# A two-layer graph attention kernel on one core: norm statistics by VectorE instead of TensorE transposes, first-layer weights by ScalarE, new issue lists

## The chip, the core and the metric

The kernel runs on one core of one Trainium2 chip. Its engines work side by side, each on its own queue: TensorE (PE in the profile, with its weight loads as PEld) multiplies matrices, VectorE (DVE) and ScalarE (ACT) work elementwise, GpSimd (POOL) does some sums, and SyncE (SP) issues nearly all of the DMAs. The metric is the device time of one execution in microseconds; the median of the runs counts.

## The reference

The input is `x` of 64 graphs x 256 nodes x 512 features and `adj` of 64 x 256 x 256, all float32. Two layers are applied, the second of which holds two attentions.

```python
# layer 0, 8 heads of 64
Q, K, V = x @ W_q + b_q, x @ W_k + b_k, x @ W_v + b_v
scores = Q K^T / 8 + a_i + c_j + b_g + log(adj + 1e-9)
x = softmax(scores) @ V + x
# layer 1
def layer_norm(x): return (x - mean) * rsqrt(var + 1e-6) * g + b
def graph_attention(x, bias, W, a_src, a_dst):
    h = x @ W                                   # split into heads
    e = leaky_relu(s_i + t_j, 0.2) + bias        # s = h . a_src, t = h . a_dst
    return softmax(e) @ h
attn = graph_attention(layer_norm(x), adj, W1, ...) + x        # 8 heads
out  = graph_attention(layer_norm(attn), adj, W2, ...) + attn  # 1 head
```

## The kernel before

One graph passes through a chain of 42 named steps, written as a Python generator `graph(b)`, which stops after each step. A list says which graph takes its next step when. In the steady part this list is `period`: an entry `(age, name)` lets the graph that is `age` graphs behind the newest take the step `name`, so five or six graphs are under way at once, each in another stage. `start` and `finish` are lists of their own for the two ends. TensorE executes in exactly the order of these lists. The other engines get an order from the scheduler of the framework, which starts what it takes to be ready; each engine then executes its queue strictly in that order.

The steps of one graph are these.

- `load`, `turn`: x and adj come in by DMA, are transposed by VectorE in blocks of 32 x 32 (L471), and lie with features on the partitions (`xT`, tiles of 128 x 4 x 256).
- `V`, `Q`, `K`: three products with 512 x 512 weights, each by a Strassen-Winograd scheme of seven block products (`winograd`; L306 and L313). `V 7`, `V 4` and the like are the last two products of a scheme. GpSimd makes its left sums (`left_factors`, L282 to L285). ScalarE copies intermediate PSUM banks (L495, L528, L607), VectorE adds (L507, L537, L545, L616).
- `scores`, `mask`, `sums 0`, `product 0`, `gather 0`: score products (L562), Exp by ScalarE out of PSUM (L569), multiplication by adj (L583) and sum over key blocks (L588) on VectorE, column sums by TensorE (L362), weighted values by TensorE (L394), and the division and the addition to the residual on VectorE (L403, L408). The inverse sums go through DRAM to reach all partitions. The residual goes to DRAM (`store`) and comes back (`fetch`).
- `tokens 1`: the reciprocal standard deviation of layer norm for each token. TensorE transposes the residual (L249), ScalarE takes the sum and the squares with accumulator (L264, L266), VectorE scales (L270), GpSimd raises to the power -0.5 (L272). The mean itself and g, b are folded into the weights once at the start (`fold_norm`).
- `V1`, `rows 1`, eight times `weights`, `sums 1`, `product 1`, `gather 1`: the first attention of layer 1. The weights are exp(leaky_relu(s+t)+adj), up to a factor that cancels: ScalarE takes Exp of adj plus 0.2 t (L647), VectorE multiplies by the larger of exp(-0.8 s) and exp(0.8 t) (L650).
- `tokens 2`, `V2`, `rows 2`, `weights 2`, twice `product 2`: the second attention with one head. The residual `X2`, in token order, is a by-product of the transposes in `tokens 2` (L264, with the constant row added by GpSimd at L669); L711 multiplies, L718 divides and adds, and L727 sends the result out.

VectorE and GpSimd also keep extremes of intermediate values (`note`, L345, L379, L380). At the end they are compared with bounds; a value outside leads to a slower plain version of the whole computation, which does not run with these inputs.

[...] In SBUF, tiles with one tag share a fixed number of slots: the layer-0 and layer-1 weights `ET` share four, and the temporary `product` of `fold_norm` uses the same four.

Of the kernel before, what the change touches and what calls it, by code (L numbers as in the profile page):

```python
# [15 lines left out]
H = 8  # L16
# [4 lines left out]
def kernel(  # L21
# [46 lines left out]
    top = const.tile([P, P + 4 * H], F32, name="top")  # L68
    bottom = const.tile([P, 4 * H], F32, name="bottom")
    added = const.tile([P, P], F32, name="added")  # L70
# [4 lines left out]
    for t in (top, bottom, added):  # L75
        nc.gpsimd.memset(t, 0.0)
# [9 lines left out]
    nc.gpsimd.memset(eights, 1.0)  # L86

# [57 lines left out]
    with ExitStack() as main:  # L145
# [13 lines left out]
        def fold_norm(name, w, g, b, sources, targets, heads):  # L159
# [9 lines left out]
            for a in (sources, targets):  # L169
                row = data.tile([P, D], F32, name="vector", tag="X2", bufs=4)  # L170
                nc.sync.dma_start(out=row, in_=a.rearrange("h d -> (h d)").partition_broadcast(P))
                vectors.append(row.rearrange("p (n f) -> p n f", n=2))
            for kk in range(2):
                blocks = w[:, kk, :4, :HD].rearrange("p (k n) f -> p k n f", n=2)
                for i, row in enumerate(vectors):
                    product = work.tile([P, 2, 2, HD], F32, name="product", tag="ET", bufs=4)
# [10 lines left out]
            left = data.tile([P, 2, KC, 32], F32, name="left", tag="X2", bufs=4)  # L187
# [10 lines left out]
            sums = data.tile([P, HD + H], F32, name="sums", tag="sums")[:, : HD + more]  # L198
# [11 lines left out]
            if name == "2":  # L210
                row = const.tile([P, D], F32, name="bw")
                nc.sync.dma_start(out=row, in_=stored[0].partition_broadcast(P))
# [31 lines left out]
        def tokens(xT):  # L244

            for t in range(NT):
                pt = ps("tr")
                for kc in range(KC):
                    nc.tensor.transpose(  # L249
                        pt[:, kc * P : (kc + 1) * P], xT[:, kc, t * P : (t + 1) * P], ident  # L250
                    )
                yield t, pt

        def rstd_of(xT, keep=None):

            total, less, squares = (
                small.tile([P, NT], F32, name=n, tag=n) for n in ("total", "less", "squares")
            )
            for t, pt in tokens(xT):
                to = pt  # L260
                if keep:
                    to, pt = keep(t), pt.rearrange("p (k a r) -> p k a r", k=KC, a=4)
                of = slice(t, t + 1)
                nc.scalar.activation(to, pt, AF.Identity, accum_out=total[:, of])  # L264
                nc.scalar.mul(less[:, of], total[:, of], -1.0 / D)
                nc.scalar.activation(  # L266
                    pt, pt, AF.Square, bias=less[:, of], accum_out=squares[:, of]
                )
            var = small.tile([P, NT], F32, name="var", tag="var")
            nc.vector.tensor_scalar(var, squares, 1.0 / D, 1e-6, ALU.mult, ALU.add)  # L270
            rstd = small.tile([P, NT], F32, name="rstd", tag="rstd")
            nc.gpsimd.tensor_tensor(rstd, var, mhalf.to_broadcast([P, NT]), ALU.pow)  # L272
            return rstd
# [68 lines left out]
        def note(v):  # L342
            n = v.shape[1]
            for kept, op in ((top[:, P:], ALU.max), (bottom, ALU.min)):
                nc.vector.tensor_tensor(kept[:, :n], kept[:, :n], v, op)  # L345

        def note_odd(v, low, high):

            bad = data.tile([P, v.shape[1]], F32, name="bad", tag="X2", bufs=4)
# [6 lines left out]
        def weight_sums(totals):  # L356
# [22 lines left out]
            nc.vector.tensor_tensor(top[:, :P], top[:, :P], pt[:, :P], ALU.max)  # L379
            nc.gpsimd.tensor_tensor(added, added, inverse, ALU.add)  # L380
            return R

        def weigh(pair, V, R, xT, bias):
# [17 lines left out]
            for q in (1, 0):  # L401
# [4 lines left out]
                for m in range(2):  # L406
                    k = 2 * q + m
                    nc.vector.scalar_tensor_tensor(  # L408
                        xT[:, k, :], both[:, m, :], bias[:, k : k + 1], xT[:, k, :],
                        ALU.add, ALU.add,  # L410
                    )
# [664 lines left out]
```

## Time and profile before

| what | value |
|---|---|
| time, median of 3 runs | 3303.91 us (3302.41 to 3306.08) |
| profiled execution: time | 3304.79 us |
| profiled execution: span of the core | 3303.0 us |
| TensorE busy | 3208.0 us, 97% |
| VectorE busy | 2488.2 us, 75% |
| ScalarE busy | 1761.0 us, 53% |
| GpSimd busy | 899.5 us, 27% |
| moved by DMA | 340.91 MB, mean 103 GB/s |
| granted TensorE clock | 0.991 of full speed |

The span reaches from the first to the last instruction of the core; the time of the execution has 1.8 us around it. Busy time of an engine is the time in which at least one of its instructions was running. The ends of matmuls are modelled, so for TensorE the distances from start to start are the safer reading. Groups of instructions are named by line: L394 is line 394 of the kernel before.

### The profile page before, as it was taken

What the parts mean: (1) busy time and instruction counts of PE and PEld (TensorE: products, weight loads), DVE (VectorE), ACT (ScalarE), POOL (GpSimd) and SP (SyncE); (2) the same over time, 40 slices, a digit from 0 to 9 for tenths busy, and PEclk for the clock granted to TensorE, in tenths of its full rate; (3) what the DMA queues carried; (4) which work ended last, traced back from release to release, by engine and by line L of the source; (5) the groups of instructions that cost most, each with busy time, mean ns of one, the idle gap of its engine ahead of it and who ended that gap; (6) DMA issues with size and microseconds to landing.
All of it is one profiled execution on the core that took longest, in us unless ns stands there. A gap on an engine that the chain in (4) does not pass through costs nothing.

```text
span 3303.0 us, 76975 instructions
## 1 busy us (share of the span) xinstructions
PE 3208.0 (97%) x29000; PEld 2686.9 (81%) x29000; DVE 2488.2 (75%) x5267; ACT 1761.0 (53%) x4807; POOL 899.5 (27%) x1244
## 2 busy tenths in 40 slices
PE   6899999999999999999999999999999999999997
PEld 4688888888888888888888888888888888888875
DVE  4667777777777777787777777777777777777775
ACT  2455555555555555555555555555555555555553
POOL 2222222322322322322322322322222222222222
PEclk8999999999999999999999999999999999999998
DMA  4324333333333333343343343343343333333322
GB/s 121 105 80 112 106 97 104 109 103 104 106 107 103 105 108 103 97 115 102 98 116 101 97 112 104 93 116 104 93 118 100 98 113 105 98 107 110 99 91 69
DMA packets 271656, 340.91 MB, mean 103 GB/s; under 512 B 108577, under 2 KB 187569, under 8 KB 271281
## 3 DMA queue, kind: packets, MB, share of 16 engines
q1 hardware_dynamic: 270512, 335.40, 36.1%
q8 instruction: 232, 3.80, 0.5%
q14 instruction: 144, 1.17, 0.1%
q10 hardware_dynamic: 768, 0.54, 0.1%
HBM read 233.48 MB, written 102.31 MB: 102 GB/s over the span
## 4 chain that ended last, share of the span: by engine, by line
PE 80%; ACT 10%; DVE 3%; DMA 3%; issue 2%; SPq 1%; POOL 1%; ACTq 0%; DVEq 0%; POOLq 0%
PE ps_a L306 18%; PE ps_num L394 12%; PE ps_a L313 10%; PE ps_b L306 9%; PE ps_sc L562 7%; PE ps_av L711 6%; ACT ET L647 6%; PE ps_c L306 4%; PE ps_su L362 4%; PE ps_b L313 3%; PE ps_tr L249 3%; ACT m L528 2%; DMA R<-kept 2%; PE ps_c L313 2%; ACT u L528 1%
## 5 line engine op out<-in xcount | busy, mean ns | idle before, releaser
L650 DVE SCALAR_TENSOR_TENSOR ET<-R,f,ET 128x256 f32<-128x256 f32 x1024 | 468.3, 496 | 243.4 <-ACT ET L647 214.7
L647 ACT ACTIVATE ET<-AT,lift 128x256 f32<-128x256 f32 x1024 | 442.6, 505 | 172.0 <-PE ps_num L394 172.0
L394 PE MATMUL ps_num<-ET,V 128*32 128x256 f32 x8192 | 466.6, 380 | 0.0
L394 PEld LDWEIGHTS ps_num<-ET,V 128*32 128x32 f32 x8192 | 264.0, 110 | 155.1 <-issue 1.3
L583 DVE TENSOR_TENSOR ET<-ET,AT 128x1024 f32<-128x1024 f32 x256 | 305.2, 1227 | 112.3 <-ACT ET L569 112.3
L569 ACT ACTIVATE ET<-ps_sc,V 128x512 f32<-128x512 f32 x512 | 303.1, 702 | 101.5 <-PE ps_sc L562 90.2
L380 POOL TENSOR_TENSOR added<-added,inverse 128x128 f32<-128x128 f32 x128 | 60.1, 470 | 891.7 <-DVE inverse L368 891.7
L306 PE MATMUL ps_a<-w,S 128*128 128x264 f32 (+1 forms) x1024 | 278.6, 395 | 9.0 <-ACT m L607 8.7
L306 PE MATMUL ps_b<-w,S 128*128 128x264 f32 (+1 forms) x1024 | 267.0, 383 | 0.1
L711 PE MATMUL ps_av<-V,ET 128*128 128x258 f32 (+1 forms) x1024 | 246.6, 385 | 5.7 <-DVE ET L699 5.7
L306 PEld LDWEIGHTS ps_a<-w,S 128*128 128x128 f32 x1024 | 183.4, 190 | 71.9 <-ACT m L607 24.8
L562 PE MATMUL ps_sc<-QT,KT 64*128 64x256 f32 x2048 | 240.0, 384 | 0.0
L562 PEld LDWEIGHTS ps_sc<-QT,KT 64*128 64x128 f32 x2048 | 193.7, 188 | 41.5 <-issue 20.9
L282 POOL TENSOR_TENSOR S<-yT 128x256 f32<-128x256 f32 x64 | 54.5, 851 | 626.2 <-PE ps_su L362 556.9
L306 PEld LDWEIGHTS ps_b<-w,S 128*128 128x128 f32 x1024 | 193.9, 189 | 31.5 <-issue 0.5
L711 PEld LDWEIGHTS ps_av<-V,ET 128*128 128x128 f32 x1024 | 187.1, 193 | 29.1 <-issue 4.6
L272 POOL TENSOR_TENSOR rstd<-var,mhalf 128x2 f32<-128x2 f32 x128 | 90.6, 708 | 284.7 <-DVE var L270 278.2
L282 POOL TENSOR_TENSOR S<-zT 128x256 f32<-128x256 f32 x63 | 45.8, 727 | 445.5 <-DVE zT L408 419.2
L403 DVE TENSOR_TENSOR ps_num<-ps_num,R 128x512 f32<-128x512 f32 x256 | 165.1, 690 | 1.7 <-DMA R<-kept 1.0
L266 ACT ACTIVATE ps_tr<-ps_tr,less 128x512 f32<-128x512 f32 x256 | 165.8, 648 | 0.1
L306 PE MATMUL ps_a<-wv,xT 128*128 128x257 f32 x512 | 142.2, 400 | 22.0 <-ACT ET L569 11.6
L669 POOL TENSOR_TENSOR X<-X,bw 128x512 f32<-128x512 f32 x128 | 159.6, 1267 | 5.7 <-ACT X L264 5.7
(167 smaller groups left out, 7022.8 us busy)
## 6 DMA issues: line engine op xcount, KB each, us to landing
R<-kept SPq DMA_DIRECT2D x128, 512.0 KB
X<-in_x_dram SPq DMA_DIRECT2D x256, 128.0 KB
kept<-xT SPq DMA_DIRECT2D x64, 512.0 KB
yT<-kept SPq DMA_DIRECT2D x64, 512.0 KB
R<-kept SPq DMA_DIRECT2D x512, 64.0 KB
kept<-yT SPq DMA_DIRECT2D x64, 512.0 KB
out_dram<-X SPq DMA_DIRECT2D x512, 64.0 KB
zT<-kept SPq DMA_DIRECT2D x63, 512.0 KB
```

Source lines behind the costliest of these rows:

```text
L266: nc.scalar.activation(pt, pt, AF.Square, bias=less[:, of], accum_out=squares[:, of])
L306: nc.tensor.matmul(to, A[:, kk, :], B[:, kk, :], start=(first and kk == 0), stop=(kk == 1), skip_group_check=not first,)
L313: nc.tensor.matmul(to[:, m * P : (m + 1) * P], B[:, kk, m * P : (m + 1) * P], A[:, kk, :], start=(first and m == kk == 0), stop=(kk == 1), ...
L394: nc.tensor.matmul(num[32 * a : 32 * a + 32, m * N : (m + 1) * N], V[:, j, a // 2, a % 2 * P + q * DH + 32 * m :][:, :32], pair[a // 2][:, ...
L403: nc.vector.tensor_tensor(both, both, R[:, q, :].unsqueeze(1).to_broadcast([P, 2, N]), ALU.mult)
L562: nc.tensor.matmul(banks[h % 2][:, o : o + N], KT[lo : lo + DH, (q + h) // 2, j * P : (j + 1) * P], QT[lo : lo + DH, (q + h) // 2, :], sta ...
L569: nc.scalar.activation(ET[:, j, i::2, :], banks[i].rearrange("p (h n) -> p h n", n=N), AF.Exp, bias=c[:, j, :],)
L583: nc.vector.tensor_tensor(ET[:, j, :, :], ET[:, j, :, :], AT[:, j, :].unsqueeze(1).to_broadcast([P, 4, N]), ALU.mult,)
L647: nc.scalar.activation(ET[:, j, h, :], AT[:, j, :], AF.Exp, bias=lift[:, j, at : at + 1])
L650: nc.vector.scalar_tensor_tensor(ET[:, j, h, :], R[q][:, h, :], f[:, j, at : at + 1], ET[:, j, h, :], ALU.max, ALU.mult,)
L669: nc.gpsimd.tensor_tensor(X2[t], X2[t], folded["2"].row, ALU.add)
L711: nc.tensor.matmul(av[:, :width], ET[:, j, t * P : (t + 1) * P], V2[:, j, n, :width], start=(j == 0), stop=(j == NT - 1),)
```

## The change

Six things are altered.

1. `rstd_of` no longer transposes on TensorE. VectorE turns the residual in 32 x 32 blocks (one instruction of 1024 elements), takes `bn_stats` of eight blocks, and one narrow product with a constant matrix `same` (48 columns) sums what belongs to one token over the partitions; ten or so narrow VectorE instructions make the variance of it. It is split in two by a generator: the first half is traced at `gather`, the second at `tokens`.
2. The first-layer weights are made as Relu on ScalarE, an addition of adj on VectorE (two heads at a time), and Exp on ScalarE, in place of Exp and L650.
3. `weigh` adds two blocks at a time; the bias is added beforehand by ScalarE on the fetched tile (`fetch_biased`).
4. The extremes are replaced by sums that ScalarE accumulates (`note`), and a further check, `skew`.
5. `X2` is made of the block-turned tile Z, plus the constant row on GpSimd, and goes through DRAM into token order. The output is scaled by ScalarE and added by GpSimd in place of L718.
6. `product` of `fold_norm` uses other slots, half of W_q is loaded by ScalarE's queue, and `start`, `period` and `finish` are new lists; graphs are up to five behind the newest in `period`.

```diff
-        def rstd_of(xT, keep=None):
...
-            for t, pt in tokens(xT):
...
-                nc.scalar.activation(to, pt, AF.Identity, accum_out=total[:, of])
-                nc.scalar.mul(less[:, of], total[:, of], -1.0 / D)
-                nc.scalar.activation(
-                    pt, pt, AF.Square, bias=less[:, of], accum_out=squares[:, of]
-                )
+        def rstd_of(xT):
+            Z = data.tile([P, 2 * KC, P], F32, name="Z", tag="Z")
+            nc.vector.transpose(
+                Z.rearrange("p b (k r) -> p k b r", k=KC), xT.rearrange("p k (b r) -> p k b r", r=32)
+            )
+            parts = small.tile([P, 2 * KC, 2, 3], F32, name="parts", tag="parts")
+            for block in range(2 * KC):
+                nc.vector.bn_stats(parts[:, block].rearrange("p h c -> p (h c)"), Z[:, block, :])
+            mean = parts[:, :, :, 1]
+            nc.vector.tensor_tensor(parts[:, :, :, 0], mean, mean, ALU.mult)
+            yield Z
+            pt = ps("st")[:, : 12 * KC]
+            nc.tensor.matmul(
+                pt, same.rearrange("p c r -> p (c r)"), parts.rearrange("p b h c -> p (b h c)"),
+                start=True, stop=True,
+            )
...
+            nc.vector.tensor_tensor(skew, skew, square, ALU.max)
+            nc.vector.tensor_scalar(var, var, 1e-6, None, ALU.add)
             rstd = small.tile([P, NT], F32, name="rstd", tag="rstd")
             nc.gpsimd.tensor_tensor(rstd, var, mhalf.to_broadcast([P, NT]), ALU.pow)
-            return rstd
+            yield rstd
...
+        def note(v, f=AF.Square):
+            n = next(slots[f])
+            unused = small.tile([P, P], F32, name="unused", tag="unused", bufs=1)[:, : v.shape[1]]
+            nc.scalar.activation(unused, v, f, accum_out=seen[:, n : n + 1])
...
+        def fetch_biased(kept, tag, bias):
+            xT = fetch(kept, tag)
+            for k in range(KC):
+                nc.scalar.activation(
+                    xT[:, k, :], xT[:, k, :], AF.Identity, bias=bias[:, k : k + 1]
+                )
+            return xT
...
-                for m in range(2):
-                    k = 2 * q + m
-                    nc.vector.scalar_tensor_tensor(
-                        xT[:, k, :], both[:, m, :], bias[:, k : k + 1], xT[:, k, :],
-                        ALU.add, ALU.add,
-                    )
+                of = xT[:, 2 * q : 2 * q + 2, :]
+                nc.vector.tensor_tensor(of, both, of, ALU.add)
...
                         nc.scalar.activation(
-                            ET[:, j, h, :], AT[:, j, :], AF.Exp, bias=lift[:, j, at : at + 1]
+                            ET[:, j, h, :], R[q][:, h, :], AF.Relu, bias=f[:, j, at : at + 1]
                         )
-                        nc.vector.scalar_tensor_tensor(
-                            ET[:, j, h, :], R[q][:, h, :], f[:, j, at : at + 1], ET[:, j, h, :],
-                            ALU.max, ALU.mult,
-                        )
+                    if h % 2 == 1:
+                        for j in range(NT):
+                            two = ET[:, j, h - 1 : h + 1, :]
+                            nc.vector.tensor_tensor(
+                                two, two, AT[:, j, :].unsqueeze(1).to_broadcast([P, 2, N]), ALU.add
+                            )
+                            for i in (h - 1, h):
+                                nc.scalar.activation(
+                                    ET[:, j, i, :], ET[:, j, i, :], AF.Exp,
+                                    bias=targets[:, j, 4 * q + i : 4 * q + i + 1],
+                                )
...
+            kept = dram.tile([P, 2 * KC, P], F32, name="kept", tag="keptz")
+            nc.gpsimd.tensor_tensor(
+                Z, Z, folded["2"].row.unsqueeze(1).to_broadcast([P, 2 * KC, P]), ALU.add
+            )
+            nc.sync.dma_start(out=kept, in_=Z)
+            yield
+            rstd = next(stats)
+            X2 = data.tile([P, NT, D], F32, name="X2", tag="X2", bufs=2)
+            for q in range(4):
+                for t in range(NT):
+                    nc.sync.dma_start(
+                        out=X2[32 * q : 32 * q + 32, t, :].rearrange("r (a f) -> r a f", a=4),
+                        in_=kept.rearrange("(a r) (t q) f -> t q r a f", a=4, t=NT)[t, q],
+                    )
...
-                    nc.vector.scalar_tensor_tensor(
-                        o[:, cols], av[:, :HD], rinv[:, t : t + 1], o[:, cols],
-                        ALU.mult, ALU.add,
-                    )
+                    weighted = work.tile([P, HD + H], F32, name="weighted", tag="kept", bufs=4)[:, :HD]
+                    nc.scalar.activation(weighted, av[:, :HD], AF.Copy, scale=rinv[:, t : t + 1])
+                    nc.gpsimd.tensor_tensor(o[:, cols], o[:, cols], weighted, ALU.add)
...
-                    product = work.tile([P, 2, 2, HD], F32, name="product", tag="ET", bufs=4)
+                    product = data.tile([P, 2, 2, HD], F32, name="product", tag="R", bufs=3)
...
         period = [
+            (1, "V4"), (2, "mask"), (5, "V2"), (5, "V2 7"), (2, "sums 0"),
+            (2, "product 0"), (5, "V2 4"), (1, "Q"), (5, "rows 2"), (4, "sums 1"),
+            (3, "weights"), (2, "gather 0"), (3, "weights"), (3, "weights"),
+            (5, "weights 2"), (3, "weights"), (0, "turn"), (1, "Q7"), (4, "product 1"),
+            (1, "Q4"), (1, "K"), (1, "K7"), (5, "product 2"), (1, "K4"), (3, "weights"),
+            (5, "product 2"), (2, "tokens 1"), (0, "V"), (1, "scores"), (3, "weights"),
+            (3, "weights"), (2, "V1"), (4, "gather 1"), (-1, "load"), (2, "V1 7"),
+            (0, "V7"), (4, "tokens 2"), (2, "V1 4"), (1, "scores"), (1, "mask"),
+            (2, "rows 1"), (2, "weights"),
         ]
```

## The prediction

> **What bounds the kernel now.** I read busy shares first, then the table of windows, then the timeline of TensorE (PE), and last what PE waits for between 300 and 3000 us.
>
> ```profile
> PE 3208.0 (97%) x29000; PEld 2686.9 (81%) x29000; DVE 2488.2 (75%) x5267; ACT 1761.0 (53%) x4807; POOL 899.5 (27%) x1244
> PE   6899999999999999999999999999999999999997
> ```
>
> PE is busy for 97%, and only the ends of the slice row dip. The windows (PE, PEld, DVE, ACT, POOL busy) say where the other 95 us lie:
>
> ```profile
> 0.00:25.00 25.00, 12.96 (x51) 9.44 (x52) 9.80 (x18) 3.79 (x9) 4.47 (x24) 1.00 0.53 139
> 25.00:50.00 25.00, 14.57 (x125) 13.34 (x123) 7.95 (x16) 4.71 (x13) 5.02 (x5) 0.90 0.65 177
> ...
> 300.00:1300.00 1000.00, 994.29 (x9052) 837.53 (x9051) 769.08 (x1626) 550.65 (x1504) 275.93 (x384) 1.00 0.37 105
> ```
>
> In the steady part PE idles 5.7 us in 1000. The first 300 us lose 49, everything after 3100 us about 33. "Busy" PE isn't PE at its peak, so I check starts. In TensorE's timeline (start, duration) one transpose step looks so:
>
> ```profile
> 1622.71 3.64 PE L394 MATMUL ps_num<-ET,V 128*32 128x256 f32 x64
> 1626.28 1.09 PE L249 MATMUL ps_tr<-ident,yT 128*128 128x128 f32 x8
> 1627.21 1.06 PE L313 MATMUL ps_a<-xT,wq 128*128 128x128 f32 x8
> ...
> 1639.20 1.06 PE L313 MATMUL ps_b<-S,wk 128*128 128x128 f32 x8
> 1640.09 1.04 PE L249 MATMUL ps_tr<-ident,zT 128*128 128x128 f32 x8
> 1640.97 1.06 PE L313 MATMUL ps_a<-S,wk 128*128 128x128 f32 x8
> ```
>
> Groups follow one another without a hole. Start to start, the transposes take 0.93 and 0.88 us, 1.81 us per graph. The page's busy figures for L249 (70.6 + 65.8 us over the run, 2.13 per graph) count overlapping tails, so I use 1.81. The chain of waits shows the score products (L562) starting at 1301.13 and at 3096.91, 36 graphs later: a period of 49.9 us. Hence PE's issue order, written by hand, is the clock, and what PE waits for in it is small:
>
> ```profile
> PE ps_a L313 <- ACT u L528: 10.9, 54, 0.5
> PE ps_a L306 <- ACT m L607: 3.8, 8, 1.3
> ```
>
> Per graph the other engines have 38.4 (DVE), 27.5 (ACT) and 13.8 us (POOL) of the 49.9.
>
> [...] the new 512-wide adds are about 690 ns, which L403 at that width also shows. [...] the POOL sums on yT have median 852 ns and reach 1238, those on zT sit at 727.
>
> **The change part by part**, per graph, for two layers.
>
> *PE.* It removes 16 transposes: -1.81 us. It adds two products of 48 columns. In the trace each f32 product leaves two records (L562: 16 calls, 32 records), a transpose one, so these are four weight loads and four short matmuls. A 128-wide pair is spaced 111 ns (L313: 0.89 us for 8). [...] 4 x 111 = 0.45 us. Bounds: 0.16 if loads hide completely (48 columns at L306's 217 ns per 257 are 41 ns), 1.0 if both steps leave a hole of 0.3 us. Net -1.36 us, period 48.5; times 64: **-87 us** (-52 to -106).
>
> *DVE.* Removed: L650 468.3, L718 121.1, L408 211, L270 75.7, L345 82, L379 29 us over the run: 987, or 15.4 per graph. Added: 8 pair adds x 0.65 = 5.2 (690 ns less the overlap that L403 has, 645); 4 adds in weigh x 0.65 = 2.6, in place of eight L408; 2 block transposes of 1024 elements: L471 takes 680 ns for 512, thus 1.18 each, 2.4; 16 bn_stats of 128 elements. [...] L379, 128 wide, is 225 ns; a pass that reduces (L181, 1221 ns for 1024) scaled down is 288. I take 250, 4.0 us; from 3.2 up to 8 if it needs two passes. Some 20 narrow instructions at the 155 to 200 ns of L683 and L345 are 3.2; the heads' sources scaled on DVE 0.2. Sum 17.6; DVE goes 38.4 -> 40.6 of 48.5 us, 84% (up to 92%). Cost nothing as long as PE is the clock.
>
> *ACT.* Removed: L647, both activations with accumulator, `less`, their reads, two small Exps: 928 us, 14.5 per graph. Added: 16 Relu and 16 Exp at 0.43 = 13.8; 8 bias additions on the fetched tile 3.5; four notes of 128 columns with accumulator (0.30 + 0.19) 2.0, two small ones 0.8; four scaled copies from PSUM at 0.47 = 1.9. Sum 22.0; 27.5 -> 35.0 us, 72%. Hidden under PE too, but here lies the new wait: before, ACT only fed DVE (Exp, then L650). Now Relu on ACT, the add on DVE, Exp on ACT: an Exp at the head of ACT waits for DVE, and behind it queue the copies of PSUM banks (L528, L607) that PE's next product needs. PE's slack there is one group, 0.87 us, and already 0.2 us short at L528. I allow 0.2 us per graph, +13 us (from 0 to 70).
>
> *POOL.* Less L669 and L380 (3.4 per graph), plus one 1024-wide addition at L177's 2.27 and four 256-wide at 0.73: 13.8 -> 15.6 us, 32%. Hidden[...]. The power of -0.5 stays where it was.
>
> *SP and DMA.* One more store of 512 KB and eight loads of 64 KB: 41 -> 50 issues a graph at some 0.43 us (L727: four in 1.74), +3.9 us. SP waits for a landing before the X2 loads, 5 to 6 us by the chain's R<-kept; behind them stand x, adj and R loads. Bytes grow from 341 to 408 MB, DMA share from 0.37 to about 0.46. X2 is read only after V2, rows 2 and weights 2, many microseconds later, and R is asked for several steps ahead of its use. Cost nothing; without that cover, up to 5 us for a late R.
>
> *Start.* In the timeline ACT stands still at the first scores, because `product` of the weight folding takes ET slots:
>
> ```profile
> 51.49 4.73 ACT L569 ACTIVATE ET<-ps_sc,V 128x512 f32<-128x512 f32 x8 [11.34 <-DVE w L181]
> 52.23 1.36 PEld L306 LDWEIGHTS ps_a<-wv,xT 128*128 128x128 f32 x4 [12.03 <-ACT ET L569]
> 52.23 2.08 PE L306 MATMUL ps_a<-wv,xT 128*128 128x257 f32 x4 [11.63 <-ACT ET L569]
> ```
>
> The change puts `product` in R's slots, idle by then, and folds later. I take **-10 us** (0 to -20); what is late next is the fold's DMA chain.
>
> *End.* The last graph's weights step has no cover: 16 Exps of 0.43 under L650 were 7.5 us, 32 activations are 13.8; an output tile passes ACT and POOL (0.47 + 0.73) instead of DVE (0.48); against it stands a shorter norm. **+7 us** (0 to +15).
>
> *Rest.* The notes at their new place, the odd-value checks and memsets at the edges: a microsecond either way.
>
> Sum against the profiled execution: 3303 - 87 + 13 - 10 + 7 = 3226 us of span, plus its own 1.8 around the span, less 0.9 to the median shown: about **3227 us**.
>
> **Rivals.**
> 1. *PE keeps the beat with small holes* (above): 3195 to 3265.
> 2. *Queue coupling eats half.* DVE at 84% and ACT at 72% answer PE late in all five winograd products of a graph, some 0.2 us each: 1 us per graph, +64 instead of +13: 3278. For it: L528's wait in 54 of 54 graphs. Against it: DVE at 77% cost PE almost nothing, and the new lists place products between Q and Q7.
> 3. *Slower: the Relu, add, Exp round trip becomes the clock.* A graph has four head pairs. If ACT stands d us per pair until DVE, busy with masks of 1.2 us, has added, ACT's period is 35.0 + 4d. It passes PE's 48.5 at d = 3.4 and the old 49.9 at d = 3.7; at d = 4.0 it is 51.0, +70 us: 3374. Against it: one mask or sum ahead costs 1.2 to 2.5, and ACT has other graphs' work.
> 4. *PE does not shrink*: transposes hidden under weight loads. The start-to-start reading speaks against it: with the additions elsewhere about 3305.
>
> **How the numbers follow.** Chances: rival 1 0.62, 2 0.22, 3 0.12, 4 0.04. A difference of 0.2%, 6.6 us, is about what can be told from no change; faster means below 3297, slower above 3311. Rival 1 and nearly all of 2 are faster: 0.83; 4 and the edge of 2 about unchanged: 0.04; slower 0.13. The likeliest is 3227. The range 3185 to 3285 takes rival 1 with the better bounds of start and PE, and most of 2.
>
> **What would show it.** PE still at or above 96%; the score products every 48.5 us; two short groups of two pairs each where L249 stood, near 0.22 us apart; DVE near 40 and ACT near 35 us per graph; the ACT wait at the first scores gone. It is wrong if PE falls under 94% in the steady windows with PE waiting for ACT copies (rivals 2 and 3), if bn_stats is far above 300 ns, or if SP waits for the Z store make R late.

## The result, and the profile after

The changed kernel takes **3262.89 us** (median of 4 runs, 3258.05 to 3264.86) against 3304.99 us (4 runs, 3302.41 to 3306.84) of the kernel before: ratio 0.9871, 95% interval 0.9854 to 0.9888. The forecast was 3227 us, 3185 to 3285. So it is 1.3% faster, inside the range, with 42 us gained of the 77 that the sum had promised. The profiled execution took 3264.86 us, its span is 3263.1 us; what follows is read from it, against the 3303.0 us before.

The page's first two parts, engine totals (busy us, share, instructions) and the slice row of TensorE:

```profile
PE 3172.2 (97%) x28232; PEld 2604.9 (80%) x28232; DVE 2700.9 (83%) x6093; ACT 2192.0 (67%) x5959; POOL 1077.0 (33%) x1315
PE   7999999999999999999999999999999999999985
```

TensorE is still at 97%, and the row dips only at its ends. VectorE has 213 us more, ScalarE 431, GpSimd 178, and hardly any of it shows in the middle. The table of windows of the changed kernel (columns as before):

```profile
25.00:50.00 25.00, 22.07 (x156) 19.28 (x158) 14.12 (x24) 9.00 (x22) 3.81 (x4) 1.00 0.59 157
300.00:1300.00 1000.00, 995.08 (x8994) 822.39 (x8994) 844.77 (x1914) 698.09 (x1910) 331.42 (x404) 1.00 0.41 128
```

TensorE idles 4.9 us in the steady 1000 (5.7 before). In the first 300 us it idles 30.8 us (48.4 before); after 3100 us it idles 49 us (31 before). **The ends cancel**: about 18 us won at the start, 18 lost at the end. What is left must come from the steady part, so I took the distance from one first-attention product (`ps_num`) to that of the next graph, over all graphs between 300 and 3100 us:

| us per graph | before | after |
|---|---|---|
| shortest distance | 49.67 | 48.75 |
| mean distance | 49.89 | 49.18 |

The shortest fell by 0.92 us (forecast: 1.36), the scatter above it grew from 0.22 to 0.43. A mean gain of 0.71 us over 64 graphs is 45 us; the two spans differ by 39.9. Counted from the first score product of the sixth graph to that of the 59th, the difference is 37.0 us, so the two ends together gain 3.

The statistics product itself is there as foreseen. TensorE's timeline of the changed kernel (start, duration, line, op):

```profile
1600.98 0.32 PE L268 MATMUL ps_st<-parts,same 128*128 128x48 f32 x2
1601.13 1.10 PE L326 MATMUL ps_a<-wv,xT 128*128 128x257 f32 x4
1602.07 1.03 PE L326 MATMUL ps_b<-wv,S 128*128 128x257 f32 x4
```

0.15 us from start to start, and the group behind it takes 0.94 where its neighbours take 0.87: 0.22 us for each product, 0.45 per graph, which is the price used. What TensorE waits for in the middle (300 to 3000 us; total, times, longest) has lost the entry of L528 and is as small as before, 10.4 us against 14.7:

```profile
PE ps_a L333 <- ACT m L525: 10.4, 16, 1.4
```

The costliest groups that are new (line, engine, op, tiles, count | busy, mean ns | idle before them):

```profile
L686 ACT ACTIVATE ET<-ET,ends 128x256 f32<-128x256 f32 x1024 | 468.2, 503 | 11.7 <-DVE ET L682 4.9
L676 ACT ACTIVATE ET<-R,f 128x256 f32<-128x256 f32 x1024 | 460.5, 501 | 85.0 <-PE ps_num L425 70.1 <-DMA R<-kept 13.6
L682 DVE TENSOR_TENSOR ET<-ET,AT 128x512 f32<-128x512 f32 x512 | 345.2, 685 | 234.7 <-ACT ET L676 234.5
L263 DVE BATCH_NORM_STATS2 parts<-Z 128x6 f32<-128x128 f32 x1024 | 227.0, 275 | 0.0
```

One `bn_stats` takes 275 ns; as they overlap, 222 ns of busy time each. The pair additions take 685 ns. The feared round trip (rival 3) is the first row: over the whole span ScalarE stood 4.9 us before an Exp because VectorE had not yet added. VectorE does the waiting instead (234.5 us for Relu), and there it costs nothing.

### The profile page after: what moved, and what is told of

Its sections match the earlier page's. It is cut to its first block, busy times and chain, and to the rows that moved or that the text cites. A ratio compares the mean times of both kernels' runs of the same rounds, so it can differ in the third digit from the quotient of the medians.

```text
span 3263.1 us, 77828 instructions
## 1 busy us (share of the span) xinstructions
PE 3172.2 (97%) x28232; PEld 2604.9 (80%) x28232; DVE 2700.9 (83%) x6093; ACT 2192.0 (67%) x5959; POOL 1077.0 (33%) x1315
## 3 DMA queue, kind: packets, MB, share of 16 engines
q14 instruction: 166, 1.36, 0.1%
## 4 chain that ended last, share of the span: by engine, by line
PE 86%; ACT 4%; DMA 3%; DVE 2%; issue 1%; SPq 0%; POOL 0%; DVEq 0%; ACTq 0%; POOLq 0%
PE ps_a L326 21%; PE ps_a L333 13%; PE ps_num L425 11%; PE ps_b L326 10%; PE ps_sc L592 7%; PE ps_av L756 7%; PE ps_b L333 6%; PE ps_c L326 5%; PE ps_su L384 4%; PE ps_c L333 3%; DMA R<-kept 2%; ACT ET L676 2%; ACT ET L686 1%; PE ps_st L268 1%; DMA zT<-kept 0%
## 5 line engine op out<-in xcount | busy, mean ns | idle before, releaser
L682 DVE TENSOR_TENSOR ET<-ET,AT 128x512 f32<-128x512 f32 x512 | 345.2, 685 | 234.7 <-ACT ET L676 234.5
L676 ACT ACTIVATE ET<-R,f 128x256 f32<-128x256 f32 x1024 | 460.5, 501 | 85.0 <-PE ps_num L425 70.1
L613 DVE TENSOR_TENSOR ET<-ET,AT 128x1024 f32<-128x1024 f32 x256 | 422.8, 1670 | 77.4 <-ACT ET L599 77.4
L686 ACT ACTIVATE ET<-ET,ends 128x256 f32<-128x256 f32 x1024 | 468.2, 503 | 11.7 <-DVE ET L682 4.9
L765 POOL TENSOR_TENSOR X<-X,weighted 128x256 f32<-128x256 f32 x256 | 211.7, 836 | 598.9 <-ACT weighted L764 598.8
L592 PE MATMUL ps_sc<-QT,KT 64*128 64x256 f32 x2048 | 258.3, 391 | 0.0
L263 DVE BATCH_NORM_STATS2 parts<-Z 128x6 f32<-128x128 f32 x1024 | 227.0, 275 | 0.0
L646 ACT ACTIVATE V<-ps_a,rstd 128x257 f32<-128x257 f32 (+1 forms) x128 | 60.0, 469 | 205.0 <-PE ps_a L326 205.0
L409 ACT ACTIVATE yT<-yT,columns 128x256 f32<-128x256 f32 x256 | 115.0, 498 | 115.9 <-DMA yT<-kept 115.8
L691 DVE TENSOR_TENSOR R<-ET 128x1024 f32<-128x1024 f32 x128 | 161.4, 1261 | 8.2 <-ACT ET L686 8.1
```

The lines of the kernel that those rows point to most:

```text
L263: nc.vector.bn_stats(parts[:, block].rearrange("p h c -> p (h c)"), Z[:, block, :])
L592: nc.tensor.matmul(banks[h % 2][:, o : o + N], KT[lo : lo + DH, (q + h) // 2, j * P : (j + 1) * P], QT[lo : lo + DH, (q + h) // 2, :], sta ...
L613: nc.vector.tensor_tensor(ET[:, j, :, :], ET[:, j, :, :], AT[:, j, :].unsqueeze(1).to_broadcast([P, 4, N]), ALU.mult,)
L676: nc.scalar.activation(ET[:, j, h, :], R[q][:, h, :], AF.Relu, bias=f[:, j, at : at + 1])
L682: nc.vector.tensor_tensor(two, two, AT[:, j, :].unsqueeze(1).to_broadcast([P, 2, N]), ALU.add)
L686: nc.scalar.activation(ET[:, j, i, :], ET[:, j, i, :], AF.Exp, bias=targets[:, j, 4 * q + i : 4 * q + i + 1],)
```

## The experiments

Four questions were open: whether TensorE's count of instructions is really the clock; where the missing 0.44 us per graph of the floor went; which part of the change is the gain; and what lengthened the end. All ratios are to the kernel before, run on the same chip. The expectations number the experiments otherwise in two places: their "third" is 7 here, and their "sixth" is 2.

**1. The statistics product twice.** The matmul of L268 is issued a second time.

```diff
+            nc.tensor.matmul(
+                pt, same.rearrange("p c r -> p (c r)"), parts.rearrange("p b h c -> p (b h c)"),
+                start=True, stop=True,
+            )
```

> The changed kernel with the narrow statistics product issued twice, one copy right behind the other, 128 groups of two matmuls more in all. Theory A (TensorE still sets the length, so each TensorE instruction is paid in full, and a group without a wait of its own costs only its spacing): 0.11 to 0.15 us x 128 = 14 to 19 us, 3277 to 3282 us, ratio to the changed kernel 1.004 to 1.006. Theory B (the gaps at hand-overs have room, or something else sets the period): less than 5 us. Theory C (each group costs its hand-over of 0.1 us as well): 27 to 32 us.

Measured: 3295.04 us, ratio 0.9973 [0.9965, 0.9982]; 32 us more than the changed kernel, and the shortest distance is 49.23 us, 0.48 more. TensorE's timeline:

```profile
1616.45 0.32 PE L268 MATMUL ps_st<-parts,same 128*128 128x48 f32 x2
1616.60 0.39 PE L272 MATMUL ps_st<-parts,same 128*128 128x48 f32 x2
1616.82 1.10 PE L330 MATMUL ps_a<-wv,xT 128*128 128x257 f32 x4
```

The second copy adds 0.22 us from start to start. 0.24 us of the shortest distance for one group of two matmuls with 48 columns: theory C. TensorE's order is the clock, in full, and the price of the new product in the forecast (0.45 us a graph) was right. The missing part lies elsewhere.

**2. The two halves of the scores side by side.** Only one entry of `period` moves.

```diff
-            (5, "product 2"), (2, "tokens 1"), (0, "V"), (1, "scores"), (3, "weights"),
+            (5, "product 2"), (2, "tokens 1"), (0, "V"), (3, "weights"),
...
-            (0, "V7"), (4, "tokens 2"), (2, "V1 4"), (1, "scores"), (1, "mask"),
+            (0, "V7"), (4, "tokens 2"), (2, "V1 4"), (1, "scores"), (1, "scores"), (1, "mask"),
```

> The changed kernel with one entry of the period moved: the first half of the scores stands directly ahead of the second half, not nine entries earlier. One hand-over at which a group's first weight load has a wait of its own falls away per graph. Theory A (the part of the forecast gain that is missing lies in these hand-overs, 0.1 us each): shortest period 48.65 instead of 48.75 us, about 6 us less in all, 3257 us. Theory B (the fixed order is tuned to VectorE's and ScalarE's queues, and any move in it costs a wait): slower by 30 us or more, with a wait of TensorE for VectorE or ScalarE once per graph. Theory C (hand-overs hide behind something): within 3 us of the changed kernel.

Measured: **3249.88 us**, ratio 0.9839 [0.9826, 0.9853], 13 us less than the changed kernel; the shortest distance is 48.50 us, 0.25 less; the mean is 48.95. It is faster than both kernels. Theory A holds, with twice the gain that it gave. TensorE's timeline, first of the changed kernel:

```profile
1605.63 2.00 PE L592 MATMUL ps_sc<-QT,KT 64*128 64x256 f32 x16
1607.56 1.16 PE L326 MATMUL ps_a<-w,yT 128*128 128x264 f32 x4
...
1615.07 2.00 PE L592 MATMUL ps_sc<-QT,KT 64*128 64x256 f32 x16
1617.00 1.13 PE L326 MATMUL ps_a<-wv,xT 128*128 128x257 f32 x4
```

and with the halves joined:

```profile
1606.74 3.73 PE L592 MATMUL ps_sc<-QT,KT 64*128 64x256 f32 x32
1610.39 1.14 PE L326 MATMUL ps_a<-wv,xT 128*128 128x257 f32 x4
```

Two halves take 1.93 us each, 3.86 together; in one piece the same matmuls take 3.65. The place where a group follows that has to wait at its first weight load (a hand-over) costs about 0.2 us, twice my 0.1. The waits of the weight loads show the same: in the changed kernel the loads of the scores stood idle 110 times between 300 and 3000 us,

```profile
PEld ps_sc L592 <- issue: 37.3, 110, 0.3
```

and joined 55 times:

```profile
PEld ps_sc L592 <- issue: 19.0, 55, 0.3
```

The kernel before had its halves side by side; the new list splits them. About half of the 0.44 us is this one entry: 0.21 in this timeline, 0.25 of the shortest distance.

**3. One entry more moved.** On top of experiment 2.

```diff
-            (5, "weights 2"), (3, "weights"), (0, "turn"), (1, "Q7"), (4, "product 1"),
+            (5, "weights 2"), (3, "weights"), (0, "turn"), (4, "product 1"), (1, "Q7"),
```

> The kernel of the sixth experiment (scores joined) with one entry more moved: product 1 directly behind sums 1, ahead of Q7, so that Q7 and Q4 are joined and one more place with a wait at its first weight load falls away; Q7 also gets 3.6 us more for VectorE's addition ahead of it. Theory A (each such place costs 0.1 us per graph, and slack ahead of Q7 takes scatter out): the shortest period 48.3 to 48.4 us, 6 to 10 us less than the sixth experiment, about 3242 us. Theory B (product 1 comes too early for the weights or its banks are not yet free): a wait of TensorE at product 1, slower than the sixth experiment by 10 us or more.

Measured: 3382.19 us, ratio 1.0242 [1.0228, 1.0256]. Theory A fell, and not as theory B said: product 1 didn't wait, Q4 did. The waits of TensorE (300 to 3000 us), then VectorE's timeline:

```profile
PE ps_a L333 <- DVE QT L567: 122.8, 53, 2.8
```

```profile
1643.53 1.64 DVE L263 BATCH_NORM_STATS2 parts<-Z 128x6 f32<-128x128 f32 x8
...
1647.16 0.42 DVE L567 TENSOR_TENSOR QT<-ps_a,m 128x256 f32<-128x256 f32 x1
```

Product 1 had been the cover between Q7 and Q4. Q4 now follows Q7 directly, and needs the addition L567, which in the changed kernel comes right behind the block transpose of Z; here it stands behind `bn_stats` and five more instructions of VectorE, and comes 1.8 us after Q7's group (1644.20 us, 1.16 us long) had ended. One hand-over saved on TensorE, 0.2 us, was paid for with 2.3 us per graph.

**4. The old lists under the new operations.** All of `start`, `period` and `finish` as before.

```diff
         period = [
-            (1, "V4"), (2, "mask"), (5, "V2"), (5, "V2 7"), (2, "sums 0"),
+            (2, "rows 1"), (1, "mask"), (0, "V"), (0, "V7"), (4, "V2 4"), (1, "sums 0"),
...
```

> The kernel after with the three lists (start, period, finish) of the kernel before; all operations as after. In the kernel after the shortest period of a graph is 48.75 us and the mean 49.17; before 49.67 and 49.87. Theory A (hand-overs): TensorE pays about 0.1 us wherever the first weight load of a step has a wait of its own, and the new period has some five more of these than the old one. Then the old lists bring the shortest period to 48.2 to 48.4 us, and the time, if the other engines follow as well, to 3225 to 3250 us. Theory B (the new lists are needed for the new operations): the old order gives VectorE too little time for bn_stats ahead of the second tokens step, or ScalarE answers late; then the shortest period may be 48.3 but the mean is above 49.2, and the time is above 3265 us.

Measured: 3968.89 us, ratio 1.2013 [1.1993, 1.2033]. Theory B holds, and it is much worse than B said: the shortest distance is 57.70 us. TensorE waits of this kernel, 300 to 3000 us:

```profile
PE ps_st L268 <- DVE parts L265: 259.2, 61, 6.8
PE ps_a L326 <- ACT m L525: 56.1, 44, 3.0
```

The old list asks for the statistics soon after the residual is complete; the chain of transpose, `bn_stats` and narrow instructions isn't done, and TensorE stands.

**5. The new lists over the old operations.** The same exchange the other way round.

```diff
         period = [
-            (2, "rows 1"), (1, "mask"), (0, "V"), (0, "V7"), (4, "V2 4"), (1, "sums 0"),
+            (1, "V4"), (2, "mask"), (5, "V2"), (5, "V2 7"), (2, "sums 0"),
...
```

> The kernel before with the three lists of the kernel after; all operations as before. Theory A: the extra hand-overs of the new period cost the old kernel as well; shortest period 50.1 to 50.3 us instead of 49.67, time 3320 to 3345 us. Theory B (lists neutral for TensorE, the small gain lies in the operations): shortest period 49.6 to 49.8, time within 10 us of 3305.

Measured: 3802.44 us, ratio 1.1519 [1.1498, 1.154]. Neither theory had a loss of this size. Once per graph, 5.2 us on average:

```profile
PE ps_a L313 <- DVE QT L537: 237.4, 46, 6.4
```

**6. The changed kernel, but the weights of layer 1 in the old way** (Exp, then larger factor and product on VectorE), with the new lists.

```diff
-                            ET[:, j, h, :], R[q][:, h, :], AF.Relu, bias=f[:, j, at : at + 1]
+                            ET[:, j, h, :], AT[:, j, :], AF.Exp, bias=lift[:, j, at : at + 1]
                         )
+                        nc.vector.scalar_tensor_tensor(
+                            ET[:, j, h, :], R[q][:, h, :], f[:, j, at : at + 1], ET[:, j, h, :],
+                            ALU.max, ALU.mult,
+                        )
...
```

> The kernel after with its new lists, in which the first-layer weights are made as before (one Exp on ScalarE, then maximum and product on VectorE) instead of Relu, addition, Exp. ScalarE has 7 us per graph less, VectorE 2 us more. Theory A: the mean period of the kernel after lies 0.42 us over its shortest, because copies for TensorE stand behind Relu and Exp on ScalarE; without them the mean falls to within 0.2 us of the shortest, and the last graphs end earlier: 3235 to 3250 us. Theory B (the spread comes from VectorE or DMA): 3255 to 3275 us, spread unchanged or larger.

Measured: 3738.52 us, ratio 1.1326 [1.1307, 1.1345]. Both theories fell: what was to be a gain became a wait once per graph. VectorE's timeline of it; it has no idle time in this stretch:

```profile
1644.75 1.19 DVE L258 STREAM_TRANSPOSE Z<-yT 128x1024 f32<-128x1024 f32 x1
...
1652.39 0.44 DVE L678 SCALAR_TENSOR_TENSOR ET<-R,f,ET 128x256 f32<-128x256 f32 x1
1652.75 0.41 DVE L564 TENSOR_TENSOR QT<-ps_a,m 128x256 f32<-128x256 f32 x1
```

and TensorE's, at the group that needed it:

```profile
1653.22 2.08 PE L333 MATMUL ps_a<-xT,wq 128*128 128x128 f32 x8 [5.29 <-DVE QT L564]
```

The addition for Q came 6.8 us after the transpose ended, behind 20 instructions, eight `bn_stats` and six of the old weights (L678) among them. In the changed kernel it follows the transpose directly. VectorE's mean load doesn't tell this; what stands in its queue at this point does.

**7. The statistics on VectorE at tokens 1 alone, the kernel before otherwise.**

```diff
+        def stats_of(xT):
...
+            stats = stats_of(xT)
+            next(stats)
             left = left_factors(xT, "yS")
             stored = store(xT)
...
-            rstd = rstd_of(xT)
+            rstd = next(stats)
```

> The kernel before, with its own lists, in which only the first of the two norms (tokens 1) takes its statistics from VectorE block transposes, bn_stats and the narrow product; tokens 2 keeps its TensorE transposes. The tile Z uses the slot of the tile X. Theory A: eight transposes (0.87 us) leave TensorE's order and two 0.08 us matmuls with about 0.07 us of hand-over come: period 49.67 to 48.95 us, time 45 us below before, about 3258 to 3265 us. Theory B (VectorE's extra 4 us per graph delay what TensorE waits for): less than 20 us gained.

`stats_of` is the new `rstd_of` of the changed kernel, in two halves.

Measured: 3431.19 us, ratio 1.0391 [1.0373, 1.0408]. Theory B holds, and it is a loss. Two waits per graph:

```profile
PE ps_st L300 <- DVE parts L297: 60.9, 52, 1.8
PE ps_a L358 <- ACT m L661: 47.1, 51, 1.3
```

The statistics come too late for the product (1.2 us), and the reciprocal deviation too late for V1 (0.9 us). Three tries to give them room by moving entries of that kernel's own period followed.

**8.** Tokens 1 behind K; V1 and V1 7 behind tokens 2.

```diff
-            (3, "product 1"), (2, "weights"), (2, "weights"), (-1, "load"), (1, "tokens 1"),
-            (0, "Q4"), (3, "gather 1"), (4, "product 2"), (2, "weights"), (1, "V1"), (2, "weights"),
-            (-1, "turn"), (1, "V1 7"), (0, "K"), (3, "tokens 2"), (0, "K7"), (4, "product 2"),
+            (3, "product 1"), (2, "weights"), (2, "weights"), (-1, "load"),
+            (0, "Q4"), (3, "gather 1"), (4, "product 2"), (2, "weights"), (0, "K"), (1, "tokens 1"), (2, "weights"),
+            (-1, "turn"), (0, "K7"), (3, "tokens 2"), (1, "V1"), (4, "product 2"), (1, "V1 7"),
```

> The kernel before with VectorE's statistics at tokens 1 alone (as in the third experiment), and with its own period altered in one place: tokens 1 moved behind K, V1 and V1 7 behind tokens 2, so that some 13 us of other TensorE work lie between the residual and the narrow product, and some 3 us between it and V1. Theory A (the third experiment's loss was the wait for the statistics, since tokens 1 came too soon): that wait goes, and with half of the transposes gone the period is shorter by 0.5 to 0.9 us: 3240 to 3275 us, ratio to the kernel before 0.980 to 0.991. Theory B (the eleven VectorE instructions fall behind others in its queue wherever the product stands in an order not made for them): still slower than the kernel before, 3330 to 3430 us.

Measured: 3732.48 us, ratio 1.1306 [1.1289, 1.1323]; theory B, and worse. The wait for the statistics is gone, two others are there:

```profile
PE ps_tr L261 <- issue: 181.2, 48, 4.1
PE ps_a L365 <- DVE QT L589: 65.9, 47, 1.9
```

For the first of them the profile names no cause. But the transposes of tokens 2 need what gather 1 writes on VectorE, and in the trace one step of them starts at 1615.56 us, while the last of gather 1's four instructions (1614.19 to 1615.84 us) runs: tokens 2 had lost V1 as its cover behind gather 1. Q7's addition stood behind the new VectorE work.

**9.** Gather 0 behind Q7, tokens 1 behind K, V1 and V1 7 ahead of tokens 2 again.

> Again the kernel before with VectorE's statistics at tokens 1 alone, its own period altered otherwise than in the eighth experiment: gather 0 (whose end puts the block transpose and eight bn_stats into VectorE's queue) stands behind Q7 instead of ahead of Q, tokens 1 behind K, and V1 and V1 7 stay ahead of tokens 2. Theory A (the losses of the third and eighth experiments were three local waits: for the statistics, of Q7 behind VectorE's new instructions, of tokens 2 for the gather that had lost its cover): no wait of TensorE above 1 us per graph is left, the period is 49.0 to 49.5 us, 3245 to 3275 us, ratio to the kernel before 0.982 to 0.991. Theory B (VectorE's load as such can't be carried by an order of this kind): over 3330 us.

Measured: 3676.49 us, ratio 1.1132 [1.1115, 1.1149]; the time of theory B. Both of those waits are gone; one is left, and TensorE stands 4.5 us per graph on average:

```profile
PE ps_a L358 <- ACT m L661: 219.5, 49, 5.3
```

V1 follows the narrow product by 1 us, and eight narrow VectorE instructions of 0.15 to 0.2 us each lie in the queue with gather 1 and weights between them.

**10.** Tokens 1 and both entries of product 2 ahead of K.

> The ninth experiment with one place more altered: tokens 1 and both entries of product 2 stand ahead of K, so that the narrow product comes about 2.5 us earlier and 5.4 us of K and K7 lie between it and V1, where there was 1 us. In the ninth experiment the product's result was ready at 1645.0 us of its trace, VectorE came to it at 1648.1 us, behind the sums of gather 1, took until 1651.7 us for ten narrow instructions with weights between them, and V1's scaled copy could start only at 1652.6 us, while TensorE waited 4.4 us. Theory A (only this wait is left, and it is one of place): it goes; period 49.1 to 49.6 us, 3245 to 3280 us, ratio to the kernel before 0.982 to 0.993. Theory B (each place that is mended moves the wait on, because the order of VectorE's queue changes with every entry): a wait of 1.5 us or more per graph at another place, over 3340 us.

Measured: 3766.32 us, ratio 1.1399 [1.138, 1.1418]. V1 waits 0.4 us now where it waited 4.4, but V2, of another graph, waits for its own deviation. TensorE's and GpSimd's timelines:

```profile
1644.61 2.08 PE L358 MATMUL ps_a<-w,S 128*128 128x257 f32 x4 [4.89 <-ACT m L661]
```

```profile
1638.03 2.49 POOL L723 TENSOR_TENSOR X<-X,bw 128x512 f32<-128x512 f32 x2
...
1643.35 0.70 POOL L284 TENSOR_TENSOR rstd<-var,mhalf 128x2 f32<-128x2 f32 x1
```

The power of -0.5 that V2 needs was ready to start at 1638.1 us, when VectorE's `var` (L282) was done, and stood behind six wide sums in GpSimd's queue until 1643.35 us. Theory B: each place that was mended moved the wait on, the last time to a third engine. That half of the statistics change gains 0.7 us per graph when its surroundings fit, as theory A of 7 to 10 says, has therefore **not been shown**; it stays open.

**11. Without GpSimd's sum on Z.**

```diff
-            nc.gpsimd.tensor_tensor(
-                Z, Z, folded["2"].row.unsqueeze(1).to_broadcast([P, 2 * KC, P]), ALU.add
-            )
```

> The changed kernel without GpSimd's addition of the constant row to the block-turned tile Z (2.39 us per graph; the row is missing in the residual of the last stage). Theory A (GpSimd's wide sums hold VectorE back: the multiplication by adj, 1.22 us at best, took 1.67 us on average and up to 3.19): the mean of that multiplication falls to about 1.25 us, VectorE is busy for about 110 us less, and TensorE's waits behind late VectorE instructions shrink, the scatter of the periods with them: 5 to 15 us less in all. Theory B (VectorE's longer instructions lie beside TensorE's work): the mean falls, the time stays within 4 us.

Measured: 3258.68 us, ratio 0.9863 [0.9848, 0.9878]: 4 us less, and the intervals overlap, so theory B. The multiplication by adj did change. In the changed kernel:

```profile
L613 DVE TENSOR_TENSOR ET<-ET,AT 128x1024 f32<-128x1024 f32 x256 | 422.8, 1670 | 77.4 <-ACT ET L599 77.4
```

without the sum:

```profile
L613 DVE TENSOR_TENSOR ET<-ET,AT 128x1024 f32<-128x1024 f32 x256 | 312.9, 1239 | 78.2 <-ACT ET L599 78.0
```

GpSimd's wide sum takes 110 us of VectorE's time, and hardly any of that reaches TensorE: the shortest distance is 48.75 us again. TensorE's waits for the copies of L525 are 14.1 us here instead of 10.4, so a gain of a few us elsewhere is not excluded. It also bounds what this contributes to experiment 2, where that mean fell to the same 1239 ns.

**12. The last graph's weights in the old way.** Only graph 63 takes the old Exp and L650.

```diff
...
+                    if b == B - 1:
+                        for j in range(NT):
+                            nc.scalar.activation(
+                                ET[:, j, h, :], AT[:, j, :], AF.Exp, bias=lift[:, j, at : at + 1]
+                            )
...
```

> The changed kernel in which the last graph alone makes its first-layer weights in the old way (Exp on ScalarE, then larger factor and product on VectorE, no Relu). Theory A (the end became longer because ScalarE has the weights of the last graph to itself, 32 Relu and Exp instructions of 0.5 us each per half, with no other graph's work beside them): TensorE's idle time after 3100 us falls by 4 to 10 us, and the time with it. Theory B (the end is longer by the order of its steps: the statistics and the waits for weights of the second layer): within 3 us of the changed kernel.

Measured: 3257.64 us, ratio 0.9871 [0.9856, 0.9886]. The median is 5 us below the changed kernel's, but the kernel before was 3 us faster beside it as well, and the ratio is the same: the times show no gain. In the profile TensorE's idle time after 3100 us is 42 instead of 49 us; in experiments 1, 2 and 11, whose last graph is that of the changed kernel, it is 46 to 51. TensorE's waits after 3100 us in the changed kernel:

```profile
PE ps_av L756 <- DVE ET L744: 22.8, 4, 8.6
PE ps_st L268 <- DVE parts L265: 8.3, 1, 8.3
```

With the old weights in the last graph:

```profile
PE ps_av L771 <- DVE ET L759: 21.5, 4, 8.5
PE ps_st L268 <- DVE parts L265: 3.1, 1, 3.1
```

In experiments 1, 2 and 11 the second of these waits is 5.8 to 7.7 us. The weights of the last graph are thus some 3 to 5 us of it: theory A in the profile, unproven in the times.

The larger part, the four waits for the second attention's weights, has another cause, and experiments 4 and 5 show which: it goes with the lists. In the kernel before it is small,

```profile
PE ps_av L711 <- DVE ET L699: 5.7, 3, 3.7
```

at the end of experiment 5 (the old operations under the new lists) it is all there,

```profile
PE ps_av L711 <- DVE ET L699: 23.3, 4, 8.4
```

and at the end of experiment 4 (the new operations under the old lists) most of it is gone:

```profile
PE ps_av L756 <- DVE ET L744: 10.0, 3, 5.3
```

The three lists were exchanged together; for the last graphs it is `finish` that counts. The old one is no cure as it stands: the end of experiment 4 has 18.2 us of waits for the first attention's weights and 13.3 for the statistics instead.

## Why the prediction was right, and where it was off

- **What bounds it**: right. Every added TensorE instruction was paid in full (experiment 1), and VectorE's 110 us less in experiment 11 bought nothing that the times can tell.
- **PE, -87 us**: the mechanism was right, the size was not. The terms of the sum hold: 1.81 us out, and 0.45 in, measured 0.44 to 0.48. The 0.45 came out in part by luck: it was worked out as 0.22 us for a pair of short products, but the pair takes 0.15 and the group behind it 0.07 more. That 48 columns are spaced like 128 was an estimate of mine, and it doesn't hold: 0.15 us for a pair against 0.22 (L313 before, 0.89 us for four). The step that failed is what the sum left at nothing: that every other group keeps the spacing that it had in the old order. The floor fell by 0.92 us, -59 us over 64 graphs. Added up from start to start over the fastest graph of each trace, the transposes are 1.80 us less and the new product 0.31 more; of the rest, with as many matmuls as before, the scores take 0.20 more, the column sums 0.11, the products into the banks `ps_a` 0.50 (0.14 of it belong to the statistics, above), those into `ps_b` 0.27 less, all others 0.03 more. So the missing 0.44 us are spacing at other places of the order. For the scores experiment 2 shows the cause; that the others are hand-overs too is likely, but not tried.
- **Jitter, +13**: the size was right, the cause only in part, so there is luck in it. Scatter above the shortest distance grew by 0.21 us per graph, 13 us; rival 2's 1 us wasn't reached. As foreseen TensorE waits for copies of PSUM banks (L525) that stand behind Relu and Exp in ScalarE's queue. But it isn't Exp that holds the queue up by waiting for VectorE. In 12 of the 16 waits, 8.3 of the 10.4 us, the Relu at the head of the queue had waited for the DMA of `R` some 4.5 us earlier, each time about 0.25 us longer than TensorE then waited. ScalarE's timeline at the longest, then TensorE's:

```profile
1047.57 2.11 ACT L676 ACTIVATE ET<-R,f 128x256 f32<-128x256 f32 x5 [1.65 <-DMA R<-kept]
...
1051.68 0.36 ACT L525 COPY m<-ps_a 128x256 f32<-128x256 f32 x1
```

```profile
1052.09 1.16 PE L333 MATMUL ps_a<-S,wk 128*128 128x128 f32 x8 [1.41 <-ACT m L525]
```

In the kernel before, `R` was read by VectorE (L650), and the Exp of ScalarE (L647) never waited for it; now its first reader shares a queue with those copies.
- **DVE, ACT, POOL**: 41.5, 34.3 and 16.3 us per graph (busy shares between 300 and 1300 us times 49.18), forecast 40.6, 35.0 and 15.6. `bn_stats` was priced 250 ns, measured 222 to 275. Relu and Exp were priced alike, an estimate of mine; measured 501 and 503 ns (L676, L686). VectorE's surplus is more than accounted for by the multiplication by adj, which GpSimd's sum on Z lengthens (110 us, 1.7 per graph): experiment 11 shows it with 1670 ns beside the sum against 1239 ns without it. The forecast's sum has no term for it, and none was needed.
- **SP and DMA**, at nothing: not quite. The DMA share is 0.41 (forecast 0.46), and no wait of TensorE in the middle names a DMA, but most of those for L525 go back to a late `R`, which the prediction had named among its signs of being wrong. It is small, 8.3 us in 55 graphs. Why `R` lands late in some graphs and not in others, by the store of Z or otherwise, was not tried.
- **Start, -10**: measured about -18. The wait of 11.3 us at the first scores is gone as foreseen, and the 25 us from 25 to 50 us alone hold 7.5 us more TensorE work; which part the new `start` has in the rest wasn't tried.
- **End, +7**: measured about +18 (49 us against 31, which the prediction had read as 33). The step that failed is that the longer first-layer weights were taken for nearly the only burden. They are some 3 to 5 us of a wait, near the 6.3 priced; the waits for the second attention's weights grew by 17 us, which the new lists bring with either set of operations (experiments 4, 5 and 12), and the sum had no term for an end in another order.
- **Rival 3 and its opposite**: the round trip cost ScalarE 4.9 us in all. A slower kernel was near all the same: with the lists or the operations alone, or with the old weights under the new lists, it is 13 to 20% slower (experiments 4 to 6). What I held for a question of load (84% of VectorE) is in these runs one of order in the queue.

By parts, the forecast -87 + 13 - 10 + 7 = -77 stands against -59 + 13 - 18 + 18 = -46; the spans differ by -40, and the 6 us between are not assigned: near the ends graphs don't pass at the steady distance.

## What to carry to other kernels

When one engine's issue order is the clock, price a change as instructions removed times their start-to-start distance (here 1.81 us per graph forecast, 1.80 measured), and then count the hand-overs of the new order as well: a group split in two cost 0.2 us here, 13 us over the run. For every other engine ask not how busy it is but what stands in its queue between the data and the instruction that the clock waits for; an order tuned for one set of operations was 15 to 20% slower with another, in both directions. So neither part of such a change can be judged alone under the order of the other. And ask what the first instruction of a busy queue reads: when a tile that a DMA brings moves to another engine, its lateness can move to whatever stands behind it there (here 8.3 of TensorE's 10.4 us of waits in the middle).

## What the runs showed of the hardware

- **After a wait of about 5 us TensorE came back at half its clock; after one of 2.3 us mostly at full.** Windows behind the waits of 5.29 us in experiment 6 and 2.28 us in experiment 3; the third number from the end is the granted clock:

```profile
1653.20:1655.00 1.80, 1.78 (x8) 1.78 (x9) 1.80 (x5) 0.02 (x1) 0.00 (x0) 0.50 0.48 109
1655.00:1657.00 2.00, 2.00 (x15) 2.00 (x14) 2.00 (x4) 0.98 (x3) 0.00 (x0) 0.73 0.18 41
```

```profile
1647.60:1648.60 1.00, 0.96 (x8) 0.96 (x9) 0.67 (x3) 1.00 (x4) 0.00 (x0) 1.00 0.22 74
```

The same eight matmuls took 1.87 and 0.99 us from start to start. In the steady part of experiments 5 and 6 all 56 waits of each, 4.5 us and longer, were followed by half the clock (mean of the next 1.5 us); in experiment 3, 45 of 56, 2.2 to 2.8 us long, by the full one and 11 by about half, which lasted 3.41 us each time. Such a long wait therefore cost more than its length: in experiments 5 and 6 holes of 5.5 and 6.0 us per graph (all rows) stand against 8.2 us more per graph in both (mean distance 58.10 against 49.89, and 57.38 against 49.18), in experiment 3 holes of 2.4 us against 2.2 (51.20 against 48.95).
- **Splitting a group of matmuls in two cost 0.2 us, though no wait of TensorE for data is there**: 3.86 against 3.65 us for the scores, with one more idle stretch of the weight loads per graph. A product of 48 columns cost 0.22 us: 0.15 for its pair of records and 0.07 in the group behind.
- **`bn_stats` on 128 f32 elements takes 275 ns, 222 ns of busy time each in a row**, not far from an elementwise maximum of that width (L379 before: 225).
- **A GpSimd sum of 1024 elements, 2.39 us long, held one VectorE multiplication per graph from 1.22 to about 3.15 us.** Between 300 and 3000 us 55 of 220 took over 3 us in the changed kernel; without the sum none took over 1.23 (experiment 11).
